# A four-layer graph network: layer 3's preparation split into four groups of nodes, its two products joined, and the last layernorm split in three

## The chip, the cores and the metric

The kernel runs on one core of a Trainium2 chip. The metric is the device time of the whole program in microseconds (us), lower is better. Before the change three runs took 574.63, 577.2 and 579.83 us; the median is 577.2 us. One more execution, the profiled one, took 574.9 us, of which the profile's span (first to last instruction) is 573.2 us. All times inside the kernel come from that one execution and are counted from the start of its span.

Engines are named as the profile names them: PE is TensorE (PEld its weight loads), DVE is VectorE, ACT is ScalarE, POOL is GpSimd, and SP is the queue that issues nearly all DMA transfers. L386 is line 386 of the kernel before.

## The reference, cut to what matters

Four layers run on 3327 nodes with 64 features and one dense adjacency matrix `adj`. Each adds its result to its input and applies a layernorm. Layer 2 has two hops; layer 3 weighs the neighbours of a node by their rank in the row.

```python
x = _layernorm(x + _L0(x))                  # adj @ x
x = _layernorm(x + _L1(x, adj, ...))        # all pairs, hyperbolic distances
# layer 2
for k in range(2):
    agg = adj @ x
    x = jnp.tanh(jnp.concatenate([agg, x], axis=1) @ W[k])
# layer 3
support = input @ weight
mask = (adj != 0)
rank = jnp.cumsum(mask, axis=1)
deg = rank[:, -1:]; k = jnp.minimum(deg, 100.)
pos = rank - (deg - k)
w = mask * jnp.where(pos > 0, 0.5 ** (k - pos), 0.0)
out = w @ support + bias
```

## The kernel before

Nodes are padded to 3328, which is 26 blocks of 128. The transposed adjacency is read in blocks of 128 rows (1664 KB each) or half rows (832 KB). Vectors that a product needs by feature are stacked: 64 features of a node of the first half and 64 of its partner in the second half fill the 128 partitions, so such a tile has 1664 columns (13 groups of 128 nodes, or four chunks of `CW` = 416). `fours` cuts the 13 groups into 4, 4, 4 and 1, `threes` into 3, 3, 3, 3 and 1.

**Order of the work.** In `layers` PE's order is the program's; during layer 2 and in layer 3's main loop DVE and ACT run in the program's order as well (`manual_schedule`), while layer 3's preparation and the last layernorm leave DVE and ACT to the scheduler. SP's queue is in order. Waits are semaphores that the tile layer sets from the tiles' readers and writers and from the reuse of a pool's buffers.

**Layer 2.** At its beginning DVE writes the normalized input `x2` in five pieces (L1323); `turned` transposes them on PE (L334) and ACT copies them into `hT`; `top` makes the left factor of the hop (PE L344, copies L374) and `bottom` adds the node's own part. Each hop sums over 26 blocks (`add`, L386) into four PSUM accumulators of 416 columns, one for each chunk. Each call of `add` is two fp32 products, each recorded as two matmuls; one block is 16 records. Six blocks stay in SBUF (`kept`: 25 to 22 for good, 21 and 20 until layer 2 ends), six are left over from the hop before (`ready`), and 14 are streamed in hop 2 through four buffers `strm` (and two more at first). The list `order` puts one kept block ahead of every few streamed ones; the last two kept blocks come at the end, chunk by chunk, each chunk followed by its tanh on ACT (L453). In hop 1 the chunks end in the order 0 to 3, in hop 2 in the order 3 to 0.

**Layer 3's preparation.** When hop 2 is done, `residual` multiplies the tanh result by the centering matrix `center` (PE L529), DVE adds `x2` (L534), ACT squares (L537), DVE sums the squares (L538); `scaled` takes the inverse root (a square root on ACT L231, then five small DVE steps L232 to L238) and multiplies (L546), which gives `x3`; `turned` transposes it (PE L553, copies L557); `factor` multiplies by the layer's weight (PE L563) and splits the fp32 result into three bf16 parts (ACT L569, DVE L570, ACT L571, POOL L572). Between these, `count` (PE L468) starts the ranks: for a block, PE adds triangular and all-ones products of the block's 0/1 mask onto two PSUM tiles `cnt`, and `read` turns the sums into bf16 weights `w` (first half of the columns on ACT L484, the other on DVE L482). `advance` moves the ranks to the next block and so waits for `read`.

**Layer 3's main loop** goes through 52 steps (two halves of the output, 26 blocks each). A step reads the ranks, makes a mask for a later block (DVE L326, from a transfer `ah` issued at L324), advances the ranks, and multiplies (`products`, PE L614; every three steps twelve more with the third bf16 part, L627). `products` runs `LEAD` = 3 steps behind the ranks. After the first half `sums_out` copies the sums (ACT L643, DVE L644), `half_out` centers them (PE L653) and does the layernorm in small pieces beside the loop. After the second half the same steps run alone, in two parts of 8 and 5 groups, and three transfers issued by SP (L674, L679) store the result.

Of the kernel before, what the change touches and what calls it, by code (L numbers as in the profile page):

```python
# [23 lines left out]
D = 64  # L24
# [42 lines left out]
STEP = float(2**7)  # L67


@with_exitstack  # L70
def kernel(
# [65 lines left out]
    w3_dg = const.tile([P, P], F32, name="w3_dg")  # L137
# [39 lines left out]
    center = const.tile([P, P], F32, name="center")  # L177
# [120 lines left out]
    def layers(ctx, x2, kept, ready, ahead_ctx, strm):  # L298
# [52 lines left out]
        x3 = xpool.tile([P, NB, D], F32, tag="x", name="x3")  # L351
        hT = cols.tile([P, HALF], F32, tag="hT", name="hT_0")
        with tc.tile_pool(
            name="l2p", bufs=2, space=PSUM, reuse_waits="tile"
        ) as l2p, tc.tile_pool(
            name="l2a", bufs=CPH, space=PSUM, reuse_waits="tile"
        ) as l2a, tc.manual_schedule(
            engines={mybir.EngineType.DVE, mybir.EngineType.Activation}
        ):
            for k in range(2):  # L360
                hw = lj
                nxt = cols.tile([P, HALF], F32, tag="hT", name=f"hT_{k + 1}")
                acc = [l2a.tile([P, CW], F32, tag="acc", name=f"acc2_{k}_{c}") for c in range(CPH)]
# [30 lines left out]

                stay = list(kept)
                others = [jb for jb in range(NB) if jb not in kept and jb not in ready]
                share = -(-len(others) // (len(stay) - 2))
                order = list(ready)
                for i, jb in enumerate(stay[:-2]):
                    order += [jb] + others[i * share : (i + 1) * share]  # L400
                blocks = {**ready, **kept}

                if k == 0:
# [14 lines left out]
                    for c in range(CPH):  # L418
                        bottom(c)

# [29 lines left out]
                for c in range(CPH) if k == 0 else reversed(range(CPH)):  # L450
                    for jb in stay[-2:]:
                        add(c, jb, jb == stay[-1])
                    nc.scalar.activation(nxt[:, c * CW : (c + 1) * CW], acc[c], AF.Tanh)  # L453

# [18 lines left out]
        def read(q):  # L473
            if q >= len(steps):
                return
            h, jb = steps[q]
            for c in range(2):
                w = l3w.tile(
                    [P, 2, CW], BF16, tag=f"w{c}", bufs=LEAD + GROUP + 2, name=f"w_{h}_{jb}_{c}"
                )  # L480
                if c:
                    nc.vector.tensor_scalar(w.bitcast(I16), cnt[c], 0.0, None, ALU.max)  # L482
                else:
                    nc.scalar.activation(w.bitcast(I16), cnt[c], AF.Relu)  # L484
                ws[q, c] = w
# [15 lines left out]
        def spread(v, n):  # L501
# [8 lines left out]
        xT = cols.tile([P, HALF], F32, tag="hT", name="xT_3")  # L510
        s12 = l3n.tile([P, NB, 2, D], BF16, name="s12")
        s3 = l3n.tile([P, NB, D], BF16, name="s3")
        rr = lj
        l3w = ctx.enter_context(tc.tile_pool(name="l3w", bufs=2, reuse_waits="tile"))
        l3c = ctx.enter_context(
            tc.tile_pool(name="l3c", bufs=1, space=PSUM, reuse_waits="tile")
        )
        cnt = [l3c.tile([P, 2, 512], F32, name=f"cnt_{c}")[:, :, :CW] for c in range(2)]

        with tc.tile_pool(name="l3t", bufs=4, space=PSUM, reuse_waits="tile") as l3t:  # L520

            def ps(name):
                return l3t.tile([P, 4 * P], F32, tag="ps", name=name)

            def residual(g, n):

                pr = ps(f"pr_h2_{g}")
                for c in range(n):
                    nc.tensor.matmul(  # L529
                        pr[:, c * P : (c + 1) * P], hT[:, (g + c) * P : (g + c + 1) * P], center,  # L530
                        start=True, stop=True,
                    )
                sl = slice(2 * g, 2 * (g + n))
                nc.vector.tensor_tensor(  # L534
                    hid[:, sl], pr[:, : n * P].rearrange("p (n d) -> p n d", d=D), x2[:, sl], ALU.add
                )
                nc.scalar.activation(sq[:, sl], hid[:, sl], AF.Square)  # L537
                nc.vector.tensor_reduce(var[:, sl], sq[:, sl], axis=AX.X, op=ALU.add)  # L538

            def scaled(part):  # L540
                sl = slice(2 * part[-1][0], 2 * (part[0][0] + part[0][1]))
                r = rsqrt_of(var[:, sl], sl.stop - sl.start)
                for g, n in part:
                    s = slice(2 * g, 2 * (g + n))
                    o = s.start - sl.start
                    nc.vector.tensor_tensor(  # L546
                        x3[:, s], hid[:, s], spread(r[:, o : o + 2 * n], 2 * n), ALU.mult
                    )

            def turned(g, n, copy):  # L550
                pt = ps(f"pt_x3_{g}")
                for c in range(n):
                    nc.tensor.transpose(  # L553
                        pt[:, c * P : (c + 1) * P],
                        by_half(x3)[:, g + c].rearrange("p h d -> p (h d)"), ident,
                    )
                copy(xT[:, g * P : (g + n) * P], pt[:, : n * P])  # L557

            def factor(g, n):

                pn = ps(f"pn_l3_{g}")
                for c in range(n):
# [136 lines left out]
        for _ in half_out(1, sums_out(1)):  # L699
            pass  # L700
# [884 lines left out]
```

## Time and profile before

| what | us |
|---|---|
| median of three runs | 577.2 (574.63 to 579.83) |
| profiled execution | 574.9 |
| its span | 573.2 |
| layer 1 and earlier | 0 to about 242 |
| hop 1 of layer 2 | about 242 to 327 |
| hop 2 of layer 2 | 327 to 407.9 |
| layer 3's preparation | 407.9 to 426.85 (first L614) |
| main loop | 426.85 to 558.4 |
| last layernorm and stores | 558.4 to 573.2 |

PE is busy for 529.3 us of the span (92%), DVE for 361.6, ACT for 275.0, POOL for 216.4. A busy PE is a modelled figure; it is read for its gaps here. The page cuts the span in 40 slices of 14.3 us, so one digit of a row is 14.3 us, and layer 3's preparation fills little more than one of them. Stages of that length are read from the timeline and from the busy time by windows.

### The profile page before, as it was taken

Reading aid. Unit: us, or ns where it says so; the run is one execution under the profiler, and the core shown is the slowest. Engines: PE = TensorE matmul, PEld = TensorE weight load, DVE = VectorE, ACT = ScalarE, POOL = GpSimd, SP = SyncE. Lnnn points to the kernel's source line nnn. Section 1 sums busy time; section 2 is a strip of 40 time slices with the busy share of each in tenths; the row PEclk is TensorE's granted clock in tenths of the full one; section 3 lists DMA queues with packets and bytes.
Section 4 is the critical chain, followed back from the end, with each engine's and each line's share of the span. In section 5 each row is a group of like instructions: output and inputs, shape, how many; then the busy total and the mean of one; then the engine's idle time right before and its main releaser. Section 6 shows DMA issues by size and latency. Waiting matters only on the chain.

```text
span 573.2 us, 7492 instructions
## 1 busy us (share of the span) xinstructions
PE 529.3 (92%) x2864; PEld 226.3 (39%) x2864; DVE 361.6 (63%) x510; ACT 275.0 (48%) x327; POOL 216.4 (38%) x134
## 2 busy tenths in 40 slices
PE   8899989999999999699999999999879999899992
PEld 5522222222222224254444444433455555555542
DVE  7899999999999998920000010300487787698733
ACT  4999999998999997330000100000453333333320
POOL 3799999999999998100000000000020000000000
PEclk9999999999999999989999999999999999999996
DMA  8977675650766653999999049996618995689701
GB/s 294 369 257 223 214 231 193 236 180 3 237 210 215 232 180 123 396 428 423 426 426 396 5 176 424 373 406 289 236 64 274 330 339 192 235 266 355 247 1 35
DMA packets 34020, 145.26 MB, mean 253 GB/s; under 512 B 10269, under 2 KB 11959, under 8 KB 28855
## 3 DMA queue, kind: packets, MB, share of 16 engines
q1 hardware_dynamic: 32295, 144.27, 68.4%
q10 hardware_dynamic: 1680, 0.43, 0.3%
q8 instruction: 24, 0.39, 0.3%
q14 instruction: 21, 0.17, 0.1%
HBM read 143.23 MB, written 0.87 MB: 251 GB/s over the span
## 4 chain that ended last, share of the span: by engine, by line
PE 63%; DVE 20%; ACT 9%; issue 3%; DMA 3%; DVEq 0%; POOL 0%; POOLq 0%; ACTq 0%
PE acc L386 24%; PE pq L910 12%; DVE v L931 12%; PE cnt L468 11%; PE acc L614 5%; ACT sg L886 3%; PE acc L627 3%; ACT pq L923 2%; DVE a L922 2%; DMA at_l<-in_adjT 2%; DVE w L482 2%; PE pn_l L344 1%; PE pr_o L653 1%; PE acc L377 1%; DVE mask L326 1%
## 5 line engine op out<-in xcount | busy, mean ns | idle before, releaser
L897 POOL TENSOR_TENSOR u<-sg,at 128x832 f32<-128x832 f32 x88 | 169.8, 1957 | 3.2 <-ACT sg L886 2.7
L910 PE MATMUL pq<-riT,ljT 64*128 64x416 f32 x416 | 100.3, 560 | 15.2 <-DVE v L931 6.3
L922 DVE SCALAR_TENSOR_TENSOR a<-pq,dl,u 128x832 f32<-128x832 f32 x104 | 111.9, 1077 | 3.0 <-PE pq L910 2.9
L923 ACT ACTIVATE pq<-pq,al,gas 128x832 f32<-128x832 f32 x104 | 104.9, 1010 | 15.2 <-DVE a L922 14.2
L931 DVE SCALAR_TENSOR_TENSOR v<-pq,a 128x832 f32<-128x832 f32 x104 | 105.7, 1016 | 1.1 <-ACT pq L923 0.8
L943 PE MATMUL acc<-v,xv 128*64 128x416 f32 x416 | 95.4, 538 | 0.1
L386 PE MATMUL acc<-at_l,lj 128*64 128x416 f32 x480 | 86.5, 514 | 1.0 <-DMA at_l<-in_adjT 1.0
L886 ACT ACTIVATE sg<-lb,rb 128x1664 f32<-128x1664 f32 (+1 forms) x53 | 87.3, 1647 | 0.1
L484 ACT ACTIVATE w<-cnt 128x832 int16<-128x832 f32 x52 | 44.8, 862 | 72.9 <-PE cnt L468 72.8
L453 ACT ACTIVATE hT<-acc 128x416 f32<-128x416 f32 x8 | 4.1, 517 | 149.4 <-PE acc L386 149.4
L572 POOL TENSOR_TENSOR s<-lj,s 128x512 bf16<-128x512 f32 (+1 forms) x4 | 3.9, 977 | 182.8 <-ACT s L571 182.8
L482 DVE TENSOR_SCALAR w<-cnt 128x832 int16<-128x832 f32 x52 | 53.2, 1024 | 26.3 <-PE cnt L468 25.0
L910 PEld LDWEIGHTS pq<-riT,ljT 64*128 64x128 f32 x416 | 31.6, 185 | 88.3 <-DVE v L931 83.0
L374 DVE COPY lj<-pn_l 128x384 f32<-128x384 f32 (+2 forms) x8 | 4.3, 542 | 86.7 <-PE pn_l L344 86.7
L468 PE MATMUL cnt<-mask,rest 128*128 128x416 bf16 x200 | 51.7, 340 | 3.3 <-ACT w L484 2.5
L386 PEld LDWEIGHTS acc<-at_l,lj 128*64 128x64 f32 x480 | 34.1, 138 | 50.6 <-issue 47.9
L468 PE MATMUL cnt<-mask,tri 128*128 128x416 bf16 x208 | 53.4, 339 | 0.1
L614 PE MATMUL acc<-w,s 128*128 128x416 bf16 x208 | 52.3, 340 | 0.8 <-DVE lj L570 0.8
L943 PEld LDWEIGHTS acc<-v,xv 128*64 128x64 f32 x416 | 20.6, 135 | 61.0 <-issue 57.7
L326 DVE TENSOR_SCALAR mask<-ah 128x1664 bf16<-128x1664 f32 x42 | 43.4, 1033 | 0.0
L386 PE MATMUL acc<-kept,lj 128*64 128x416 f32 x192 | 35.2, 513 | 0.0
L897 POOL TENSOR_TENSOR u<-sg,kept 128x832 f32<-128x832 f32 x16 | 30.9, 1965 | 3.8 <-ACT sg L886 3.8
(266 smaller groups left out, 391.8 us busy)
## 6 DMA issues: line engine op xcount, KB each, us to landing
at_l<-in_adjT SPq DMA_DIRECT2D x26, 1664.0 KB, 12.3
at<-in_adjT SPq DMA_DIRECT2D x44, 832.0 KB, 4.9
ah<-in_adjT SPq DMA_DIRECT2D x42, 832.0 KB, 6.6
bt_l<-in_adjT SPq DMA_DIRECT2D x8, 1664.0 KB, 11.1
kept<-in_adjT SPq DMA_DIRECT2D x6, 1664.0 KB, 8.7
lb<-lf_rows SPq DMA_DIRECT2D x2, 384.0 KB, 4.5
ljT<-ljT SPq DMA_DIRECT2D x4, 128.0 KB, 6.4
out<-hid SPq DMA_DIRECT2D x2, 256.0 KB, 5.8
```

The lines of the kernel that those rows point to most:

```text
L326: nc.vector.tensor_scalar(mask[q], at, 0.0, None, ALU.not_equal)
L386: nc.tensor.matmul(acc[c][h * D : (h + 1) * D, :], hw[:, slot(jb), :], blocks[jb][:, o : o + CW], start=c not in begun, stop=last, skip_gr ...
L468: nc.tensor.matmul(cnt[c][:, e, :], mat, mask[q][:, of], start=start, stop=(mat is tri), skip_group_check=True,)
L482: nc.vector.tensor_scalar(w.bitcast(I16), cnt[c], 0.0, None, ALU.max)
L614: nc.tensor.matmul(acc[h, c][:, e, :], s12[:, slot(jb)].rearrange("p t d -> p (t d)"), ws[q, c][:, e, :], start=first, stop=last,)
L886: nc.scalar.activation(sg[:, :, of], lbs[:, :, of], AF.Sigmoid, bias=rb[:, sl : sl + 1])
L897: nc.gpsimd.tensor_tensor(u, sg[:, :, of], at[:, :, of], ALU.mult)
L910: nc.tensor.matmul(pq[:, h, :], ljT[h != jb // NBH][rows, of], riT[rows, ch * CW : (ch + 1) * CW], start=True, stop=True,)
L922: stt(a_s[t], pqs[t], dl[:, one], us.pop(t), op0=ALU.add, op1=ALU.mult)
L923: nc.scalar.activation(pqs[t], pqs[t], AF.Square, bias=al[:, one], scale=gas[:, one])
L931: stt(w, pqs.pop(t), CUBIC_REST, a_s.pop(t), op0=ALU.add, op1=ALU.mult)
L943: nc.tensor.matmul(accs[cp, ci][h * D : (h + 1) * D, :], xv[:, slot(jb), :], w[:, h, :], start=(jb == order[0]), stop=(jb == order[-1]),)
```

## The change

Three parts, and what follows from them.

1. **Storage.** The four accumulators of layer 2 are no longer four tiles of one bank: they are the two halves of each of the two tiles `cnt`, which layer 3 uses for its ranks. The transposed input of layer 2 lies in the buffer of an earlier layer (`x3 = xc`), which becomes `x3` later; it is kept because the residual is now added in transposed form.
2. **Layer 3's preparation by groups, beside hop 2's last chunks.** In hop 2 blocks 24, 23 and 22 are the last ones (three instead of two), and 14 streamed blocks stand between three kept ones. `chunk_end` finishes a chunk; `with_x2` adds the transposed input to the tanh result on DVE; `finish` multiplies a group of nodes by `both_m`, which is `center` beside `center` times the weight, so that one product of 256 columns gives residual and factor (the product of the two matrices is made once in hop 1). `squares`, `sums` and `roots` give the inverse root, now by nine small DVE steps with no square root on ACT; `factor` and `x3_of` scale the two halves. The groups are A (10 to 12), B (7 to 9), C (4 to 6) and E (0 to 3). All of it, and the three first steps of the ranks, is written out in one order for PE, DVE and ACT. The bf16 parts of C and E and their `x3` are made in the first steps of the main loop.
3. **Ends of the halves.** In the last block of a half the products of the first column half are closed before those of the second are begun; `sums_out` of the first half stands after the reads of the next step. The last layernorm runs in parts of 6, 4 and 3 groups in a fixed order, and two of its four stores are issued by ACT.

```diff
-    w3_dg = const.tile([P, P], F32, name="w3_dg")
+    both_m = const.tile([P, 2 * P], F32, name="both_m")
+    w3_dg = both_m[:, P:]
-    center = const.tile([P, P], F32, name="center")
+    center = both_m[:, :P]
...
-        x3 = xpool.tile([P, NB, D], F32, tag="x", name="x3")
-        hT = cols.tile([P, HALF], F32, tag="hT", name="hT_0")
+        x2T = x3.rearrange("p n d -> p (n d)")
+        hT = x2T
+        l3c = ctx.enter_context(
+            tc.tile_pool(name="l3c", bufs=1, space=PSUM, reuse_waits="tile")
+        )
+        cnt = [l3c.tile([P, 2, 512], F32, name=f"cnt_{c}")[:, :, :CW] for c in range(2)]
+        acc = [cnt[c // 2][:, c % 2, :] for c in range(CPH)]
...
                 stay = list(kept)
+                if k:
+                    stay.sort(key=lambda jb: jb >= NB - EARLY)
+                n_end = 3 if k else 2
+                stay, end = stay[:-n_end], stay[-n_end:]
...
+                    pw = l2p.tile([P, 4 * P], F32, tag="pt", name="pw_3")[:, :P]
+                    nc.tensor.matmul(pw, center, w3_dg, start=True, stop=True)
+                    nc.scalar.copy(w3_dg, pw)
...
+                def chunk_end(c):
+                    for jb in end:
+                        add(c, jb, jb == end[-1])
                     nc.scalar.activation(nxt[:, c * CW : (c + 1) * CW], acc[c], AF.Tanh)
...
+        def with_x2(c):
+            of = slice(c * CW, (c + 1) * CW)
+            nc.vector.tensor_tensor(nxt[:, of], nxt[:, of], x2T[:, of], ALU.add)
+        def finish(l3t, i):
+            g, n = parts[i]
+            pt = l3t.tile([P, 4, 2 * P], F32, tag="both", name=f"both_{i}")
+            for k in range(n):
+                nc.tensor.matmul(
+                    pt[:, k, :], nxt[:, (g + k) * P : (g + k + 1) * P], both_m,
+                    start=True, stop=True,
+                )
...
+        def squares(i):
+            nc.scalar.activation(halves(sq[:, slots(i)]), both[i][0], AF.Square, scale=0.125)
+        def sums(i):
+            nc.vector.tensor_reduce(var[:, slots(i)], sq[:, slots(i)], axis=AX.X, op=ALU.add)
+        def roots(sl):
...
+            nc.vector.tensor_scalar(v, v, LN_EPS, None, ALU.add)
+            nc.vector.tensor_scalar(
+                y.bitcast(I32), v.bitcast(I32), -0.5, ROOT_BITS, ALU.mult, ALU.add
+            )
+            tt(t, v, y, ALU.mult)
+            tt(t, t, y, ALU.mult)
+            stt(p, t, -10.0 / 3.0, t, op0=ALU.add, op1=ALU.mult)
+            stt(y, p, 5.0, y, op0=ALU.add, op1=ALU.mult)
+            tt(t, v, y, ALU.mult)
+            tt(t, t, y, ALU.mult)
+            stt(y, t, -3.0 / 0.140625, y, op0=ALU.add, op1=ALU.mult)
...
+        with tc.tile_pool(name="l3t", bufs=2, space=PSUM, reuse_waits="tile") as l3t:
+            chunk_end(3)
+            with_x2(3)
+            chunk_end(2)
+            with_x2(2)
+            finish(l3t, A)
+            squares(A)
+            chunk_end(1)
+            sums(A)
+            roots(slots(A))
+            factor(A)
+            with_x2(1)
+            finish(l3t, B)
+            squares(B)
+            x3_of(A)
+            sums(B)
+            first_part(A)
+            count(1, tri, 0, True)
+            read(1, 0, False)
+            rest_of(A)
+            chunk_end(0)
+            roots(slots(B))
+            with_x2(0)
+            other_parts(A)
+            finish(l3t, C)
+            count(0, tri, 0, True)
+            advance(1, 0)
+            squares(C)
+            read(0, 0, False)
+            factor(B)
+            x3_of(B)
+            first_part(B)
+            sums(C)
+            finish(l3t, E)
+            hid_out(C)
+            advance(0, 0)
+            rest_of(B)
+            read(1, 1, True)
+            squares(E)
+            hid_out(E)
+            advance(1, 1)
+            read(0, 1, False)
+            other_parts(B)
+            sums(E)
+            advance(0, 1)
+            roots(slice(0, 2 * sum(parts[C])))
+            read(1, 2, False)
+            advance(1, 2)
+            read(0, 2, False)
+            advance(0, 2)
+            factor(C)
+            factor(E)
...
-            if c and (len(later) == 2 * GROUP or last):
+            if last or c and len(later) == 2 * GROUP:
                 for ql, cl in later:
+                    if last and cl != c:
+                        continue
...
+            added(parts[0])
+            added(parts[1])
+            summed(parts[0])
+            added(parts[2])
+            summed(parts[1])
+            summed(parts[2])
+            r = rsqrt_of(v, NBH)
+            for s, queue in zip(parts, (nc.sync, nc.scalar, nc.sync)):
...
+        with_step = {
+            LEAD: lambda: (first_part(C), rest_of(C), other_parts(C)),
+            LEAD + 1: lambda: (first_part(E), rest_of(E), other_parts(E)),
+            LEAD + 2: lambda: x3_later(C),
+            LEAD + 3: lambda: x3_later(E),
+        }
+        for q in range(LEAD, len(steps) + LEAD + 1):
+            read(0, q, False)
+            read(1, q, True)
+            if q == NB + LEAD:
+                accT = sums_out(0)
+            masks(q + AHEAD)
+            with_step.pop(q, lambda: None)()
```

## The prediction

> **What bounds the kernel now.** I read first the page's slices and its chain by engine, then the chain in order of time, then busy time by windows of 10 us, then the timeline where the change acts.
>
> ```profile
> PE   8899989999999999699999999999879999899992
> PE 63%; DVE 20%; ACT 9%; issue 3%; DMA 3%; DVEq 0%; POOL 0%; POOLq 0%; ACTq 0%
> ...
> 259.92 67.19 PE acc L386 x384
> 378.58 12.23 DMA at_l<-in_adjT
> 390.86 17.00 PE acc L386 x96
> 407.88 4.15 DMA ah<-in_adjT
> 413.41 1.28 ACT L231
> 415.40 1.02 DVE w L482
> ...
> 380.00:390.00 10.00, 9.87 (x56) 3.64 (x52) 0.00 (x0) 0.00 (x0) 0.00 (x0) 1.00 1.01 431
> 410.00:420.00 10.00, 6.32 (x41) 4.09 (x40) 9.58 (x25) 5.74 (x10) 0.00 (x0) 1.00 0.56 234
> 440.00:478.00 38.00, 38.00 (x242) 20.14 (x240) 29.33 (x31) 12.88 (x16) 0.00 (x0) 1.00 0.93 334
> ```
>
> PE sets the time. Hop 1 is one unbroken run of 384 records from 259.92: whatever delays its beginning delays all. Hop 2's end hangs on a transfer (the chain goes through `at_l`; in the row 380 to 390 the columns after span and five engines are PE clock 1.00, DMA share 1.01 and 431 GB/s). In layer 3's preparation PE is busy 6.32 of 10 us and DVE 9.58. In the main loop PE is full.
>
> The places of the change in the timeline:
>
> ```profile
> 244.01 0.55 PE L334 MATMUL pt_x<-ident,x 128*128 128x128 f32 x3 [0.32 <-DVE x L1323]
> 245.00 0.74 DVE L1323 TENSOR_TENSOR x<-pm,bx 128x384 f32<-128x384 f32 x2
> 245.31 1.48 PE L344 MATMUL pn_l<-w_dg,hT 128*128 128x128 f32 x6 [0.75 <-ACT hT L338]
> ...
> 407.88 0.52 ACT L453 ACTIVATE hT<-acc 128x416 f32<-128x416 f32 x1 [0.88 <-PE acc L386]
> 408.45 3.17 PE L529 MATMUL pr_h<-center,hT 128*128 128x128 f32 x26 [0.62 <-ACT hT L453]
> 426.85 0.51 PE L614 MATMUL acc<-w,s 128*128 128x416 bf16 x2 [0.76 <-DVE lj L570]
> 432.86 1.25 PE L627 MATMUL acc<-w,s 128*64 128x416 bf16 x12
> 493.94 0.51 PE L468 MATMUL cnt<-mask,rest 128*128 128x416 bf16 x2 [1.44 <-ACT w L484]
> 559.10 3.12 PE L653 MATMUL pr_o<-center,accT 128*128 128x64 f32 x26 [0.69 <-ACT accT L643]
> 568.11 0.49 SPq L679 DMA_DIRECT2D out<-hid  x1
> ```
>
> The reader is to see PE's brackets: 0.62 us from a chunk's last product over its tanh to PE's next product; 1.44 us lost between the halves.
>
> [...] the trace has 0.115 us per weight load. [...] the trace held 1.00 over PE's gap of 2.27 us before 417.44[...].
>
> **The change part by part**, against the profiled execution (span 573.2, 574.9 us in all, 2.3 below the median of 577.2). In the built program I read the order and the waits.
>
> *Hop 1's beginning.* PSUM is laid out anew, and the second three transposes of `x2` now wait for DVE's last piece of `x2`, not its second. DVE ends it at 245.74, the transposes then take 0.55, so the `top` product begins at 246.4, not 245.31: +1.1 (0 to 1.6; PE runs unbroken behind it, nothing hides it). The product of the two matrices is two records of 0.14 (six `pn_l` in 0.83 at 252.09): +0.3; its ACT copy (0.27) lies beside products.
>
> *Hop 1's end.* Two chunks now share a tile, and waits are kept for whole tiles: chunk 1's first product waits for chunk 0's tanh, chunk 3's for chunk 2's. Twice the 0.62: +1.25 (0 to 1.5). On PE everything is queued behind; the tanhs of chunks 1 and 3 are covered by `top`. So hop 2, with its stream, begins 2.65 later.
>
> *Hop 2's stream.* Before, the last streamed block landed 11.8 after its issue at 387.0 (398.8), and its products ended at 402.08. PE now reaches it one kept block (2.8) sooner, and has to wait for it. The streamed block that follows the second kept one frees its buffer 2.8 sooner, and that can refill dips: the windows of 2 us from 368 to 378 moved 0.68 to 0.87 MB where 0.87 is full, 0.6 MB or 1.4 us in all. I take 0.9 (0 to 1.4). Landing 398.8 + 2.65 - 0.9 = 400.6, products until 403.5: +1.4 against 402.08 (0.9 to 2.3). Call this moment T.
>
> *From T to the main loop.* Before: two kept blocks (5.6), 26 records of L529 (3.17), 13 transposes (about 2), 26 records of L563 (1.42 + 1.95 = 3.4), ranks; first L614 at T + 24.77, the first group of twelve L627 at T + 30.78. After: three kept blocks (8.4), 26 records of 256 columns. [...] I take 0.12, as the 26 of L529 show, 3.1 in all (bound 5.7). The order written out, all in us after T: chunk 3 to 2.1; its tanh to 2.7; chunk 2 waits for it (shared tile), to 4.8; A's product to 5.55; chunk 1 to 7.65; B's product to 8.4; chunk 0 to 10.85. On DVE, A: squares at 6.1 (ACT 0.5), sum 0.55, nine root steps at the 0.21 spacing of L232 to L238 (1.9), factor 0.6 (to 9.25); then two adds and scalings of 0.59, B's sum, A's remainder, B's roots to 13.1, `with_x2(0)` to 13.6, B's factor and `x3` to 14.6. E's product needs the buffer that `x3_of(B)` frees, so PE idles from 12.65 to 14.65: this wait is new, and behind it on PE stand the rank steps. E's product to 15.6. From here ACT and PE alternate: squares, `hid_out`, four reads of 0.86 on ACT, rank steps of 0.70; first L614 at T + 21.95. In the next steps ACT and DVE carry the parts of C and E (ACT 0.48 + 0.48 and 0.6 + 0.6, DVE 0.55 and 0.7, twice `x3_later`); `read` of column half 0 then comes late twice, 0.65 and 1.1. First L627 group at T + 29.3, 1.5 sooner than before. From there PE is the bound again. Bounds: -5 if PE's largest gaps close (E's 2.0, the two late reads 1.75), +2.5 if each of the 27 DVE steps ahead of E's product costs 0.1 more and a record of the joint product 0.17.
>
> Sum to here: +1.4 - 1.5 = -0.1.
>
> *Other moved steps.* POOL's four third parts (0.43 to 1.16) have an idle queue. SP: the first four `ah` transfers no longer wait for hop 2's last chunk, only for the last streamed block; they land before DVE reads them at T + 21. ACT's table load for the square root (1.28 at 413.41) moves into `half_out` of the first half, where ACT sat idle 2.35; without that cover it would cost a read, up to 1.
>
> *Between the halves.* The reads stand ahead of `sums_out`, so the 1.44 gap closes, and 0.3 of small waits before it; the late squares (PE's 0.44 at 500.9) grow by about 0.25. PE does two rank steps (1.4) while DVE copies (1.08). -1.7 (-2.0 to -1.0).
>
> *The end.* Six records (four L627 of 0.10, two L614 of 0.18: 0.76) leave the way of the first half's copy, which L653 waits for; the second copy (DVE 1.08) then binds after six of 13 groups: -0.35. Three parts cost DVE two more small steps and a later last sum, +0.3. The last store was issued at 568.11 behind two of SP's; now ACT issues two: -0.5. -0.5 in all (-1.0 to +0.4).
>
> Sum: -0.1 - 1.7 - 0.5 = -2.3, thus 572.6 against 574.9, and by the same step 574.9, rounded 575, against the median of 577.2.
>
> **The rivals.**
> *The groups hide everything.* For it: PE's two largest waits after T, 3.75 in all, stand behind single steps of other engines, and DVE is free before 6.1. Against: DVE works without pause from T + 6.1 to T + 14.6. It gives -5 in place of -1.5, and a stream that recovers 1.4 in place of 0.9: 571.
> *The root chain binds.* Ahead of E's product stand 27 DVE steps, 18 of them root steps of which each needs the one before. If a step costs 0.3 more than its row (raw-bit steps and groups of six columns have no row of their own), E's product moves from T + 14.65 to T + 22.7 and every read behind it as far: +8 on -2.3, slower: 583. It decides as soon as E's product starts later than T + 17, where the forecast's gain is gone. Against: L232 to L238 stand 0.21 apart in the trace at 13 columns.
> *The overlap does not take place.* Hop 2's end hangs on the transfer; PE waits out what the moved kept block should cover, hop 1's 2.65 stays whole, the stream's 0.9 and the preparation's 1.5 are lost: +2.4 on -2.3, which is the time before: 577. For it: a stream at its ceiling for 40 us. Against: the kept products have the same work in either place, and PE has gaps to take it.
>
> **How the numbers follow.** Forecast 0.40 (573 to 577.5); all hidden 0.20; no overlap 0.21; root chain 0.19. Eight in ten: 570 to 582, which leaves out a third of all hidden and some half of the root chain. One per cent, 5.8 us, is about what a measurement of this kernel can tell from no change: within it are the forecast, no overlap, two fifths of all hidden and half of the root chain: same 0.78, faster 0.12, slower 0.10.
>
> **What would show it.** In the new profile: `pn_l` of hop 1 beginning about 1.1 later; PE gaps of 0.6 inside both hops' ends; last `at_l` products waiting on DMA; PE idle before E's product, ended by DVE; first L627 group some 29 us after the last streamed block; no gap of 1.4 between the halves. Wrong it would be if hop 1 ends where it did, or if DVE's root steps stand wider than 0.25 apart.

## The result, and the profile after

Twelve runs of the changed kernel have a median of 576.05 us (575.07 to 577.64), twelve of the kernel before 577.09. The ratio of after to before is 0.9987, with a 95% interval of 0.997 to 1.0004: no change that can be told. The profiled execution took 575.8 us, its span 573.9 (before: 574.9 and 573.2).

From the page of the changed kernel, PE's row of the slices and the chain by engine:

```profile
PE   8899989999999999689999999998989999999992
PE 63%; DVE 19%; ACT 8%; DMA 4%; issue 4%; POOL 0%; DVEq 0%; POOLq 0%
```

PE still sets the time, with the same share of the chain as before (63%). From the chain in order of time (start, length, what it was):

```profile
261.45 63.02 PE cnt L395 x360
...
388.09 12.89 DMA at_l<-in_adjT
401.02 5.13 PE cnt L395 x28
...
409.07 1.49 PE both L558 x6
```

Hop 2's end still hangs on a transfer (12.89 us of the chain go through `at_l`). The last line is the new joint product: six records in 1.49 us, 0.25 each. Busy time by windows (PE, PEld, DVE, ACT, POOL, then PE clock, DMA share, GB/s):

```profile
380.00:390.00 10.00, 9.51 (x57) 3.67 (x54) 0.00 (x0) 0.00 (x0) 0.00 (x0) 1.00 1.01 431
410.00:420.00 10.00, 10.00 (x50) 5.21 (x49) 8.06 (x29) 5.15 (x11) 1.12 (x1) 1.00 0.39 162
440.00:478.00 38.00, 38.00 (x241) 20.15 (x240) 29.31 (x31) 12.89 (x16) 0.00 (x0) 1.00 0.93 320
```

In the row 410 to 420 PE is now full, where it was busy for 6.32 us before: the groups do fill the hole. But more of PE's work lies in that row now (chunks of a third kept block, products of 256 columns in place of 128), and the end of the preparation is no sooner. In the main loop PE is full in both. The timeline at the places of the change:

```profile
243.62 0.52 PE L339 MATMUL pt_x<-ident,x 128*128 128x128 f32 x3 [0.57 <-DVE x L1441]
246.24 0.83 PE L339 MATMUL pt_x<-ident,x 128*128 128x128 f32 x3 [2.11 <-DVE x L1441]
246.87 1.48 PE L349 MATMUL pn_l<-w_dg,xc 128*128 128x128 f32 x6
...
325.07 3.01 PE L395 MATMUL cnt<-kept,lj 128*64 128x416 f32 x16 [0.62 <-ACT hT L471]
328.70 1.62 PE L395 MATMUL cnt<-kept,lj 128*64 128x416 f32 x8 [0.62 <-ACT hT L471]
330.25 1.16 PE L349 MATMUL pn_l<-w_dg,hT 128*128 128x128 f32 x8
...
401.02 3.01 PE L395 MATMUL cnt<-at_l,lj 128*64 128x416 f32 x16 [0.97 <-DMA at_l<-in_adjT]
403.87 2.27 PE L395 MATMUL cnt<-kept,lj 128*64 128x416 f32 x12
406.75 2.31 PE L395 MATMUL cnt<-kept,lj 128*64 128x416 f32 x12 [0.62 <-ACT hT L471]
409.00 1.56 PE L558 MATMUL both<-both_m,hT 128*128 128x256 f32 x6
...
419.36 1.96 PE L558 MATMUL both<-both_m,hT 128*128 128x256 f32 x8
...
427.69 0.52 PE L689 MATMUL acc<-w,s 128*128 128x416 bf16 x2
435.45 1.25 PE L704 MATMUL acc<-w,s 128*64 128x416 bf16 x12
496.33 3.01 PE L729 MATMUL pr_o<-center,accT 128*128 128x64 f32 x26
506.26 1.25 PE L704 MATMUL acc<-w,s 128*64 128x416 bf16 x12
559.73 3.12 PE L729 MATMUL pr_o<-center,accT 128*128 128x64 f32 x26
568.64 0.57 ACTq L770 DMA_DIRECT2D out<-hid  x1
```

The places before that these are measured against:

```profile
243.17 0.52 PE L334 MATMUL pt_x<-ident,x 128*128 128x128 f32 x3 [0.57 <-DVE x L1323]
327.04 1.16 PE L344 MATMUL pn_l<-w_dg,hT 128*128 128x128 f32 x8
402.08 5.76 PE L386 MATMUL acc<-kept,lj 128*64 128x416 f32 x32
495.35 3.01 PE L653 MATMUL pr_o<-center,accT 128*128 128x64 f32 x26
505.23 1.25 PE L627 MATMUL acc<-w,s 128*64 128x416 bf16 x12
```

The work ahead of the first transposes (243.62; 243.17 before) is the same in both, and the fourteen traces of this study, all with that work unchanged, have their first transposes between 243.17 and 244.68; these 0.45 us are not put down to the change. From there, by stage, in the two traces (T is the end of the last streamed block, where the first product of the last kept blocks begins: 402.08 and 403.87):

| stage | before | after | difference | forecast |
|---|---|---|---|---|
| first transposes to hop 2's first product | 83.87 | 86.63 | +2.76 | +2.65 |
| first transposes to T | 158.91 | 160.25 | +1.34 | +1.4 |
| T to the first group of twelve (L627, L704) | 30.78 | 31.58 | +0.80 | -1.5 |
| that group to the group after the halves (505.23, 506.26) | 72.37 | 70.81 | -1.56 | -1.7 |
| that to the end of the span | 67.97 | 67.64 | -0.33 | -0.5 |

The last four rows make +0.25 (the first row is part of the second), where the forecast had -2.3: all but 0.3 of the difference lies in the preparation. The loss up to T and the gains from the middle of the main loop on came nearly as forecast; the preparation's +0.80 turns their sum of -0.55 into a small loss.

### The profile page after: what moved, and what is told of

It is laid out like the page before. It is cut to its first block, busy times and chain, and to the rows that moved or that the text cites. A ratio compares the mean times of both kernels' runs of the same rounds, so it can differ in the third digit from the quotient of the medians.

```text
span 573.9 us, 7452 instructions
## 1 busy us (share of the span) xinstructions
PE 529.7 (92%) x2827; PEld 223.3 (39%) x2827; DVE 364.6 (64%) x528; ACT 276.7 (48%) x329; POOL 216.9 (38%) x134
## 4 chain that ended last, share of the span: by engine, by line
PE 63%; DVE 19%; ACT 8%; DMA 4%; issue 4%; POOL 0%; DVEq 0%; POOLq 0%
PE cnt L395 22%; PE pq L1028 12%; DVE v L1049 12%; PE cnt L491 11%; PE acc L689 6%; DMA at_l<-in_adjT 4%; ACT sg L1004 3%; PE acc L704 3%; ACT pq L1041 2%; DVE a L1040 2%; PE pn_l L349 1%; PE both L558 1%; PE pr_o L729 1%; PE cnt L386 1%; PE idle L864 1%
## 5 line engine op out<-in xcount | busy, mean ns | idle before, releaser
L395 PE MATMUL cnt<-at_l,lj 128*64 128x416 f32 x480 | 86.5, 513 | 2.1 <-DMA at_l<-in_adjT 2.1
L506 ACT ACTIVATE w<-cnt 128x832 int16<-128x832 f32 x54 | 46.5, 864 | 72.3 <-PE cnt L491 72.3
L471 ACT ACTIVATE hT<-cnt 128x416 f32<-128x416 f32 x8 | 4.1, 517 | 146.0 <-PE cnt L395 146.0
L618 POOL TENSOR_TENSOR s<-sq,s 128x384 bf16<-128x384 f32 (+1 forms) x4 | 4.1, 1025 | 185.9 <-ACT s L617 185.9
L504 DVE TENSOR_SCALAR w<-cnt 128x832 int16<-128x832 f32 x50 | 51.2, 1023 | 25.4 <-PE cnt L491 25.0
L395 PEld LDWEIGHTS cnt<-at_l,lj 128*64 128x64 f32 x480 | 34.0, 137 | 51.4 <-issue 46.4
L395 PE MATMUL cnt<-kept,lj 128*64 128x416 f32 x192 | 36.1, 515 | 1.9 <-ACT hT L471 1.9
```

What stands on the lines that cost most here:

```text
L395: nc.tensor.matmul(acc[c][h * D : (h + 1) * D, :], hw[:, slot(jb), :], blocks[jb][:, o : o + CW], start=c not in begun, stop=last, skip_gr ...
```

## Experiments

All ratios below are to runs of the kernel before that were made beside those of the experiment (medians of 576.72 to 576.97 us); the changed kernel stands at 0.9987.

**1. Hop 1's and hop 2's waits taken away.** PSUM is laid out as before and neighbouring chunks no longer share a tile:

```diff
-            tc.tile_pool(name="l3c", bufs=1, space=PSUM, reuse_waits="tile")
+            tc.tile_pool(name="l3c", bufs=1, space=PSUM, side="right", reuse_waits="tile")
...
-        acc = [cnt[c // 2][:, c % 2, :] for c in range(CPH)]
+        acc = [cnt[c % 2][:, c // 2, :] for c in range(CPH)]
```

> The changed kernel with PSUM laid out as before (the pool of the ranks on the right side) and chunks 0 and 2 in one tile, 1 and 3 in the other, so that no two neighbouring chunks share one. Theory (hop 1's side effects are real costs): the first product L349 begins about 1.1 sooner, hop 1's last chunks lose no 0.62, hop 2's first L349 comes 2.3 to 2.4 sooner than in the changed kernel, the stream follows it in full since its transfers are released by PE, chunk 2 in hop 2 loses no 0.62 either; in all -2.3 to -3.0 against the change, about 573.0 to 573.8 us, -3.3 to -4.0 against before. Rival (the transfers of hop 2 are the bound whatever PE does before): the end of the last streamed block stays, and the time moves by less than 0.7, 575.4 to 576.1 us.

It took 571.84 us (571.45 to 572.44, 6 runs), ratio 0.9912 (0.9887 to 0.9937). The same kernel measured once more:

> waits_undone once more: its first six runs lay between 571.45 and 572.44 and its profiled run had no dip of the granted clock between 244 and 250, where before and after the change have one (worth 1.28 us of that run). If this belongs to the kernel: 571.5 to 572.5 again, ratio 0.991; if it was chance: 572.3 to 573.5, ratio 0.992 to 0.994.

571.75 us (570.82 to 571.92, 5 runs), ratio 0.9903 (0.9881 to 0.9926). This is the best version of the study, about 5 us below the kernel before and outside the interval of the changed kernel. The timeline of the second one:

```profile
243.25 0.52 PE L339 MATMUL pt_x<-ident,x 128*128 128x128 f32 x3 [0.57 <-DVE x L1441]
244.09 0.55 PE L339 MATMUL pt_x<-ident,x 128*128 128x128 f32 x3 [0.32 <-DVE x L1441]
245.38 1.47 PE L349 MATMUL pn_l<-w_dg,xc 128*128 128x128 f32 x6 [0.75 <-ACT xc L343]
...
321.70 5.76 PE L395 MATMUL cnt<-kept,lj 128*64 128x416 f32 x32
327.39 1.16 PE L349 MATMUL pn_l<-w_dg,hT 128*128 128x128 f32 x8
...
397.77 3.01 PE L395 MATMUL cnt<-at_l,lj 128*64 128x416 f32 x16 [0.98 <-DMA at_l<-in_adjT]
400.61 4.36 PE L395 MATMUL cnt<-kept,lj 128*64 128x416 f32 x24
404.90 1.56 PE L558 MATMUL both<-both_m,hT 128*128 128x256 f32 x6
...
431.36 1.25 PE L704 MATMUL acc<-w,s 128*64 128x416 bf16 x12
```

The bracket of 2.11 is 0.32 again, the three of 0.62 are gone. T stands 157.36 after the first transposes (400.61), 2.89 sooner than in the changed kernel, so the stream followed PE in full, and the rival of a fixed stream falls. The first L704 group is at T + 30.75, 0.83 sooner than in the changed kernel, and just where the kernel before had it (30.78), though one more kept block now lies behind T; T itself is 1.55 sooner than before. The waits cost more than their brackets: chunks 3 and 2 took 4.29 us (400.61 to 404.90) against 5.13 with the wait between them (403.87 to 409.00), so a bracket of 0.62 cost 0.84. The time of the runs fell by more (0.75 to 0.84%, 4.3 to 4.8 us) than these two stretches of the trace together (2.89 + 0.83 = 3.7) and than the 2.3 to 3.0 expected. The granted clock can hold the rest: its median over the runs is 0.9875 and 0.989, against 0.985 in the changed kernel, and 0.01 of it goes with 3.6 us (end of the next section), 0.9 and 1.4 us here. It dipped after the transposes in the second trace (0.50 between 246 and 248) and not in the first (1.00 throughout), where T stands 156.16 after them. No run tested the clock alone.

**2. The two halves of that edit alone.** Only the line with `side="right"`, and only the line with `acc`:

> The changed kernel with PSUM laid out as before (the pool of the ranks on the right side), the shared tiles left as they are. Theory: the transposes of x2 wait for DVE's second piece again, the first L349 begins 1.1 sooner against the first transpose, and nothing behind takes it back: about 1.1 less than the changed kernel, ratio to before near 0.997, 574.5 to 575.5 us. Rival (absorbed by hop 2's transfers): 0.9987, no change against the changed kernel.

> The changed kernel with chunks 0 and 2 in one tile, 1 and 3 in the other, PSUM's layout left as changed. Theory (from waits_undone's trace, where a wait of 0.62 cost 0.75 to 0.84 with the refill behind it): two waits in hop 1 and one in hop 2, 2.2 to 2.5 less than the changed kernel, ratio near 0.994 to 0.995, 573.2 to 574.2 us. With side_only's gain it has to add up to that of waits_undone, 3.3 to 3.6, and more only if the TensorE clock after x2's transposes is higher there.

The layout alone: 575.18 us, ratio 0.997 (0.9957 to 0.9983); in its trace the first L349 begins 2.13 after the first transposes (changed kernel 3.25, before 2.14), and T comes 1.14 sooner. The tiles alone: 574.09 us, ratio 0.9949 (0.9929 to 0.9968); its first L704 group is at T + 30.74. Against the changed kernel they make 0.17 and 0.38%, together 0.55% or 3.2 us, just under the 3.3 to 3.6 expected. The layout's 0.17% alone is inside the intervals of the runs and rests on the trace. That both at once gave somewhat more is within the intervals too. With the layout the same in both, hop 1's two kept blocks took 7.36 us with the two waits (321.88 to 329.24 in the layout's trace) and 5.69 without (321.70 to 327.39 above): 1.67 for two, 0.84 each.

**3. Only the middle.** The kernel before, with the reads ahead of `sums_out` and a column half closed before the other:

```diff
-            if c and (len(later) == 2 * GROUP or last):
+            if last or c and len(later) == 2 * GROUP:
                 for ql, cl in later:
+                    if last and cl != c:
+                        continue
...
-                later.clear()
+                later[:] = [ql for ql in later if last and ql[1] > c]
                 if last:
-                    high(q, 0)
-                    high(q, 1)
+                    high(q, c)
...
                 read(q)
+                if q == NB + LEAD:
+                    accT = sums_out(0)
...
-                if q == NB + LEAD - 1:
-                    accT = sums_out(0)
```

> The kernel before with only the change between the halves: reads ahead of the sums, and a column half's products closed before the other's begin. Theory: the gap of 1.44 closes and the small waits with it, -1.7 (-2.0 to -1.0) by the first product after the halves, and the last copy starts 0.35 sooner at the end: 575.0 to 575.5 us against 577.1. Rival (PE or ACT is late elsewhere by the same amount): 577.1, no change.

574.26 us (572.47 to 575.91, 11 runs), ratio 0.9959 (0.994 to 0.9977). The middle alone thus stands below the whole change (0.9987), with intervals that just overlap. From its timeline:

```profile
428.85 0.51 PE L614 MATMUL acc<-w,s 128*128 128x416 bf16 x2 [0.76 <-DVE lj L570]
...
495.74 3.01 PE L654 MATMUL pr_o<-center,accT 128*128 128x64 f32 x26
501.30 0.51 PE L468 MATMUL cnt<-mask,rest 128*128 128x416 bf16 x2 [0.44 <-ACT w L484]
559.14 3.12 PE L654 MATMUL pr_o<-center,accT 128*128 128x64 f32 x26
```

From the first L614 to `pr_o` are 66.89 us, 68.50 before (426.85 to 495.35): -1.61. From there to the second `pr_o` are 63.40, 63.75 before: -0.35. These are close to the forecast's -1.7 and -0.35, and the 0.35 belongs to this part, not to the last layernorm. The runs are 2.5 us below those of before, somewhat more than the two together and than the 1.6 to 2.1 expected.

**4. The middle and the last layernorm.** The same with `last_out` in place of the last `half_out`:

```diff
-        for _ in half_out(1, sums_out(1)):
-            pass
+        with tc.manual_schedule(engines={mybir.EngineType.DVE, mybir.EngineType.Activation}):
+            last_out(1, sums_out(1))
```

> The same, and the last layernorm in three parts with two stores on ACT; layer 2 and layer 3's preparation stay as before. Theory: the three parts gain between 0 and 0.3 (the changed kernel ran them 0.27 later at the last sum and its last store came no sooner): 574.7 to 575.5 us; and then storage and preparation together cost about 0.5 to 1.3 in the changed kernel, being its 576.05 less this. Rival (the preparation gains the 1.5 that I had forecast and the end loses it): 576 to 577.5 us here.

574.82 us (22 runs), ratio 0.9968 (0.9953 to 0.9984): the last layernorm in three parts gains nothing that can be told. And the other way round, the best version with the two parts as before. As built it leaves out the store of the last, partly filled group of 127 nodes:

```diff
-        last_out(1, sums_out(1))
+        pinned.close()
+        for _ in half_out(1, sums_out(1)):
+            pass
```

> waits_undone with the last layernorm in two parts and all stores on SP, as before the change. Theory (the three parts gain nothing: middle_end came out at 0.9968 against middle_only's 0.9959): -0.5 to +0.3 against waits_again, no difference that can be told. If the three parts are worth the 0.5 that I forecast: 0.3 or more slower than waits_again; the time from the last L704 record to the end of the span tells it closer than the total.

571.65 us, ratio 0.99 (0.9876 to 0.9925), no difference to the best version either, with the reserve that one store is missing. In its trace the last multiplication begins 7.22 us after `pr_o` (556.50 to 563.72), with three parts 7.50 (555.64 to 563.14): +0.28, the forecast's +0.3. What the two stores on ACT give back is read from the traces before and after the change: from `pr_o` to the end of the span 14.10 and 14.17. The forecast's -0.5 for the stores came as some -0.2.

**5. The joint product at half its width.** My explanation of the missing 2.3 was the price of a record: 0.12 forecast, 0.25 seen. The product was cut to its first 128 columns, which leaves the layer's weight out of the computation:

```diff
-                    pt[:, k, :], nxt[:, (g + k) * P : (g + k + 1) * P], both_m,
+                    pt[:, k, :P], nxt[:, (g + k) * P : (g + k + 1) * P], center,
...
-                pt[:, :n, o : o + P].rearrange("p n (h d) -> p n h d", h=2) for o in (0, P)
+                pt[:, :n, o : o + P].rearrange("p n (h d) -> p n h d", h=2) for o in (0, 0)
```

> The changed kernel with the joint product cut to its first 128 columns; the factor is then taken from the same columns, so the layer's weight is left out. Theory (a record of the joint product costs 0.24, [...]and lies on PE's path): 26 records at 0.12 to 0.14 in place of 0.24, and the first L704 group 2 to 3 us after the last streamed block sooner than the changed kernel's 31.58; about 573.0 to 574.2 us. Rival (DVE's and ACT's steps are the bound in the preparation): PE waits longer for ACT and DVE instead, the first L704 group moves by less than 0.5, 575.5 to 576.1 us.

It missed: 575.33 us (22 runs), ratio 0.9981 (0.9969 to 0.9993), against the changed kernel no difference that can be told. A record did fall to 0.14 (six of them from 409.79 to 410.65), but the first L704 group came only 0.81 sooner, at T + 30.77 (T is 404.66 here): less than the 2 to 3 of the theory, more than the 0.5 of the rival. PE's timeline shows where the gain went:

```profile
420.18 1.13 PE L558 MATMUL both<-both_m,hT 128*128 128x128 f32 x8 [1.83 <-DVE xc L591]
```

E's product starts at T + 15.52, as in the changed kernel (T + 15.49), now behind a wait of 1.83 for DVE's `x3_of(B)`. So the wait that I had forecast there (2.0) exists, hidden by PE's own lateness. A second theory: PE and DVE reach E's product at the same moment, and only shortening both helps.

DVE's side of it, from A's sum to the end of `x3_of(B)`, first in the changed kernel, then with the narrow product:

```profile
411.12 0.55 DVE L570 TENSOR_REDUCE l_var<-sq 128x6 f32<-128x384 f32 x1 [0.86 <-ACT sq L567]
418.67 0.55 DVE L591 SCALAR_TENSOR_TENSOR xc<-both,root_y 128x384 f32<-128x384 f32 x1
```

```profile
411.28 0.55 DVE L570 TENSOR_REDUCE l_var<-sq 128x6 f32<-128x384 f32 x1 [0.24 <-ACT sq L567]
419.49 0.55 DVE L591 SCALAR_TENSOR_TENSOR xc<-both,root_y 128x384 f32<-128x384 f32 x1
```

The narrow product of A lets DVE begin sooner as well: T + 6.62 in place of T + 7.25. But the chain then takes 8.76 us in place of 8.10, since one root step of B takes 0.82 in place of 0.17; it ends together with an instruction of POOL (shown in the last section). So some 0.65 of the wait of 1.83 is this collision, and the narrow product alone shows less than it is worth without it.

**6. Shorter roots, alone and with the narrow product.** The last three of the nine root steps are left out:

```diff
-            tt(t, v, y, ALU.mult)
-            tt(t, t, y, ALU.mult)
-            stt(y, t, -3.0 / 0.140625, y, op0=ALU.add, op1=ALU.mult)
```

> The changed kernel with six root steps in place of nine for each group: the second refinement of the inverse root is left out of the computation. It takes 0.6 us of DVE's work out of each of three root chains. Theory A (PE alone is the bound of the preparation): E's product starts where it did, T + 15.5 (T: end of the last streamed block), the first L704 group stays at T + 31.6. Theory B (PE and DVE come to E's product at the same moment, so that shortening one alone gives little): the same for E's product, T + 15.4 to 15.5, since PE's own records reach it then; the first L704 group at T + 31.0 to 31.6. Rival C (DVE's chain is the bound, as half_width suggests when read alone): E's product 1.2 sooner, the first L704 group at T + 30 or sooner.

> Both cuts at once: the joint product at 128 columns (the layer's weight is left out) and six root steps in place of nine. Theory B: now both arms are shorter and the wait of 1.83 us ahead of E's product falls to 0.6 or so; E's product starts at T + 14.2 (1.2 sooner than in either single cut), the first L704 group at T + 29.0 to 29.8, against 30.8 with the half width alone and 31.6 in the changed kernel; 573.5 to 574.3 us. Theory A: no difference from the half width alone, T + 30.8. Rival D (neither arm; the alternation of ACT and PE behind E's product sets the main loop's beginning by itself): T + 30.8 as well, and E's product sooner without effect.

Shorter roots alone: 576.15 us (20 runs), ratio 0.9983 (0.9969 to 0.9996), against the changed kernel nothing that can be told. Both cuts: 573.89 us (15 runs), ratio 0.9948 (0.993 to 0.9965). PE at E's product with both cuts (T is 404.75):

```profile
418.78 1.13 PE L558 MATMUL both<-both_m,hT 128*128 128x128 f32 x8 [0.35 <-DVE xc L588]
```

| kernel | E's product | wait for DVE ahead of it | first group of L704 |
|---|---|---|---|
| changed | T + 15.49 | 0 | T + 31.58 |
| narrow product | T + 15.52 | 1.83 | T + 30.77 |
| short roots | T + 15.41 | 0 | T + 31.15 |
| both | T + 14.03 | 0.35 | T + 29.00 |

Alone the cuts give 0.81 and 0.43, together 2.58. The figures are those that the second theory gave beforehand. But the sum of both is exceeded by 1.34, and about half of this is the collision with POOL: with both cuts no step of B's roots takes longer than 0.17 (415.67 to 416.84), while the narrow product alone loses 0.65 on one. The remaining 0.7 speaks for two arms of nearly equal length. No run moved POOL's work alone.

**7. Two kept blocks at the end in place of three.** In the changed kernel and in the best version:

```diff
-                n_end = 3 if k else 2
+                n_end = 2
```

> The changed kernel with two kept blocks after the last streamed one, as before the change, in place of three; one kept block (2.8 us of PE) goes back among the streamed ones. In the changed kernel PE lost 0.49, 0.61 and 0.97 = 2.07 us waiting for streamed blocks. If the transfers set T and the third block is cover that isn't needed after T: T is 0.7 to 1.5 later, PE's waits for the stream fall to 0 to 0.7, each chunk is 0.7 shorter, DVE's chain begins 1.4 sooner after T, and the first L704 group comes -0.7 to 0 us against the changed kernel: 575.3 to 576.1 us. If PE alone were the bound: -2.0, 574.0. If the third block is needed beside the preparation (my forecast's cover): the first L704 group 0.7 or more later, 576.8 us or more.

> waits_undone with two kept blocks at the end in place of three. By the same reasoning -0.7 to 0 against waits_undone's 571.84: 571.1 to 571.9 us; if the third block is needed as cover, 572.5 or more. Against before this tells also whether waits_undone's gain of 0.88 per cent comes again in other runs: 0.989 to 0.992 expected.

577.98 us (22 runs), ratio 1.0023 (1.001 to 1.0035), and 573.54 us (16 runs), 0.9945 (0.9926 to 0.9963): about 2 us slower than their counterparts in both. My expectation missed; the case "needed as cover" holds. PE's timeline of the first one:

```profile
405.36 1.57 PE L395 MATMUL cnt<-kept,lj 128*64 128x416 f32 x8
...
420.13 1.97 PE L558 MATMUL both<-both_m,hT 128*128 128x256 f32 x8 [1.99 <-DVE xc L591]
...
436.22 1.25 PE L704 MATMUL acc<-w,s 128*64 128x416 bf16 x12
```

T comes 1.7 us later, measured from the first transposes (243.38 to 405.36, 161.98 against 160.25), and the shorter chunks leave PE waiting 1.99 for DVE. Four chunks shorter by 0.7 each take 2.8 us of PE's work away behind T, but the first L704 group comes only 0.72 sooner (T + 30.86 against T + 31.58). So the third kept block lies for the most part beside DVE's work, as the change meant it to, and the rival that the overlap does not take place falls. The two stretches make +1.0 of the 2 us; the rest is not shown (0.7 of it would go with a median clock of 0.983 against 0.985).

## Why the prediction was right

It said 575.0 us (570 to 582) and most likely no change; the runs gave 576.05, no change. The effects at both ends of the change were foreseen, one in between was not, and that the time lies only 1.05 off is in part luck: the sum of the steps was -2.3, the same stages of the two traces make +0.25, and the median fell by 1.0 through something that the sum does not contain (the end of this section). The rival without overlap gave 577, just as near. Point by point:

- *Hop 1's beginning* (+1.1): 3.25 against 2.14 us between first transposes and L349, +1.11, and undone by the layout alone.
- *The product of the two matrices* (+0.3): 0.31, from 261.07 to 261.38.
- *Hop 1's end* (+1.25, at most 1.5): right in mechanism, mis-sized. The two waits cost 1.67, 0.84 each: I priced the bracket of 0.62, and the distance between the products is 0.2 more.
- *Hop 2's stream* (T later by 1.4): +1.34 after the first transposes. PE's waits on `at_l` at the end are there (0.61 and 0.97).
- *From T to the main loop* (-1.5): this step failed, +0.80. The term is the 26 records of the joint product, "I take 0.12" (the bound of 5.7 for all 26 was my estimate, not shown by the trace), read from L529: its records have 128 columns, those of the joint product 256. They cost 0.25 in groups A to C and 0.23 in E, 3.1 us more in all. So PE comes to E's product at T + 15.49 in place of T + 12.65 (some 2.3 of this is the records of A to C, the rest the chunks and the wait ahead of chunk 2), and E's own product takes 1.80 in place of 0.95. The wait of 2.0 that I drew ahead of E's product was therefore not seen. DVE was late too, by 0.7: `x3_of(B)` ended at T + 15.35 (419.22) against T + 14.65. It worked as fast as drawn (8.10 from A's sum on, forecast some 8.05; the 0.59 for a step of 416 columns was my estimate, and the four of L551 took 0.58 to 0.59) but began at T + 7.25 in place of T + 6.6, behind A's longer product and the longer wait ahead of it. E's start 0.84, own length 0.85, and 0.6 in the alternation behind it make the 2.3. The experiments add what the trace alone didn't say: a record of 0.14 brings only 0.81 by itself, since DVE's chain is then the later one, 0.65 of it through what I read as a collision with POOL (the root step of 0.82 in place of 0.17), whose parts I had costed at nothing. With both arms short the first group came at T + 29.0, near the forecast's T + 29.3.
- *Between the halves* (-1.7): -1.56, and -1.61 alone.
- *The end* (-0.5): -0.40 up to the second `pr_o`, +0.07 from there. The -0.5 for ACT's stores was too much by 0.3.

Of the rivals, "the overlap does not take place" gave nearly the measured time by a wrong mechanism: hop 1's 2.76 had shrunk to 1.34 at T, and the third kept block is hidden (experiments 1 and 7). The ceiling that it names is the DMA share: 0.93 to 1.01 in each window of 10 us from 340 to 390 in the trace of before. "The root chain binds" needed E's product later than T + 17; it came at T + 15.49, and nearly all root steps of A and B stand 0.20 apart. "The groups hide everything" would have put the first group near T + 25.8; even with both arms short it came at T + 29.0.

By the step sums the profiled execution should have been 0.25 slower in what the change touches, and the medians say 1.0 faster. A part of this lies in the kernel before, whose profiled execution was 2.2 below its median of 577.09. The old preparation has a gap of 2.3 us on PE, and behind that gap the granted clock fell in two of the three traces with it. Busy time by windows of the middle and end experiment:

```profile
416.00:420.00 4.00, 1.57 (x7) 1.18 (x7) 3.89 (x16) 0.92 (x3) 0.00 (x0) 0.69 0.11 47
420.00:424.00 4.00, 4.00 (x16) 2.64 (x14) 2.18 (x4) 1.13 (x2) 0.00 (x0) 0.50 0.00 0
```

The clock is 0.69 and 0.50 (0.97 and 0.60 in the same windows of the middle alone), and from the first `pr_h` to the first L614 are 20.90 us there and 19.91 in the middle alone, where the trace of before, at 1.00, has 18.40. Of eleven traces with the new preparation one has such a dip: that of the best version with two kept blocks, 0.57 between 416 and 420, behind a wait of 1.99 (the other trace with this wait has 1.00). Over the 48 runs of before that stood beside the first experiments, 0.01 of mean clock goes with 3.6 us, and the changed kernel's median clock is 0.985 against 0.983: 0.7 us. That the new preparation avoids these dips fits these numbers; no run tested it alone. The forecast read a granted clock of 1.00 in the trace of before, took the gap for harmless and left the point out.

## What to carry to other kernels

Before counting a new overlap as gain, list what its storage makes wait: two lines that place tiles in PSUM were worth 4 to 5 us here, most of what the change could gain. Price such a wait by the distance between the products on both sides of it and not by its idle bracket (0.84 against 0.62). Where two engines arrive together, a cut on one can show almost nothing in the time: look for the wait that appears in its place, read step by step what the other engine does in it (here a third of it was one step that took 0.82 us beside an instruction of POOL), and cut both before calling either harmless.

## What the runs showed of the hardware that was not expected

- An fp32 product's record with 128 weight columns took 0.12 to 0.14 us for 128 moving columns (26 in 3.17 us in L529 before, six in 0.86 with the narrow product) and 0.23 to 0.25 for 256 (six in 1.49, eight in 1.80), 0.105 more both in A's six records and in E's eight. Hop 2's records of 416 columns stand 0.178 apart (16 from 401.02 to 403.87), by which 128 columns would take 0.055 and 256 columns 0.11, an estimate. A weight load took 0.115 (26 in 2.98 us, the loads of L529 before). So at 256 columns a record is about as long as load and columns together (0.225 by these figures); at 128 columns it stays under their sum of 0.17. How the two share the time inside a record is not shown.
- Root steps of 0.17 us took 0.82 to 0.86 where a subtraction on POOL had just begun (0.86 in the changed kernel at 423.75, behind E's product). DVE's and then POOL's timeline in the experiment with the narrow product:

```profile
417.58 0.82 DVE L585 TENSOR_TENSOR root_e<-root_e,root_y 128x6 f32<-128x6 f32 x1
```

```profile
417.47 0.91 POOL L618 TENSOR_TENSOR s<-sq,s 128x384 bf16<-128x384 f32 x1 [172.76 <-ACT s L617]
```

The step ends at 418.40, POOL at 418.38. The two steps of 0.86 end in the same way: at 424.61 in the changed kernel and at 424.60 with the narrow product, where POOL's instruction ends at 424.59 and 424.57. That the step stood still until POOL was done is my reading of these three places; no run moved POOL's work.
- The dip of the granted clock after `x2`'s transposes (between 244 and 252) is in 13 of 14 traces, not always at the same place, with 0.50 to 0.56 in the lowest window of 2 us; in one (the first of the best version) it is missing, and the clock is 1.00. In the preparation, too, much the same gap came with a dip and without: behind PE's 2.28 us in the old one the clock fell to 0.60 and to 0.50 in two traces and held 1.00 in the third (2.27), with PE busy for 1.78, 1.57 and 2.26 of the 4 us from 416 to 420; behind 1.99 us in the new one it fell to 0.57 in one trace of two. What decides is not shown by these runs. The forecast went by the one trace at 1.00, and that was too little to call the gap harmless.
